# Four chained attention layers on one core: layer 2's chunks turned in 32x32 blocks, statistics in 64x64 tiles, the last chunk stored in one go

## The chip, the cores and the metric

The kernel runs on one core of one Trainium2 chip. The metric is the device time of one execution in microseconds (us). Before the change it is 2960.8 us, the median of 3 runs (2960.5 to 2961.66). One further execution was recorded by the hardware profiler; all durations and positions below come from that one.

The engines are called by their names or as the profile has them: TensorE (PE for products, PEld for weight loads), VectorE (DVE), ScalarE (ACT), GpSimd (POOL) and SyncE (SP, which issues most of the transfers). L1284 is line 1284 of the kernel before.

## The reference: what is computed

Four images x of 64x64 positions and 64 channels, all fp32, go through four attention layers, each on the result of the one before. Each has a softmax over all 4096 positions (1024 pooled ones in layer 1).

```
layer 0:  q, k, v = x Wq + bq, x Wk + bk, x Wv + bv;   x = gamma * softmax(q k^T) v + x
layer 1:  theta = x w_theta, phi, g = maxpool2(x w_phi), maxpool2(x w_g)      (spectrally normed weights)
          x = x + sigma * (softmax(theta phi^T) g w_o + b_o)
layer 2:  xn = group_norm(x, 32 groups, eps 1e-5), x read as (B, C, H, W); its last axis is projected:
          q, k, v = xn Wq^T + bq, ...;   o = softmax(q k^T / 8) v;   x = x + o Wp^T + bp
layer 3:  h = group_norm(x, 8 groups over channels, eps 1e-3)
          x = h + softmax((h wq + bq)(h wk + bk)^T / 8) (h wv + bv) wp + bp
```

## The kernel before, in words

**Tiling.** Each image is kept as a tile of 128 partitions by 2048 columns; the two halves of 64 partitions are two sets of tokens with 64 channels each. TensorE works as four tiles of 64x64. An attention layer goes over 4 chunks of queries (512 columns in each half) and, for every chunk, over 32 blocks of keys. `first(u)` in `attention` makes the scores of one block (L1249, four 64x64 products of 512 columns, into an `s` buffer of PSUM), ScalarE takes their exponentials into a `p` tile (L1254), VectorE adds the `p` tiles up for the softmax sums (`zacc`, L1260), and `then(u)` adds p times v into two accumulators (L1284). An fp32 product shows as two records in the profile, so four products are two groups of four records. There are two `s` buffers (two banks each), four accumulator banks and 14 `p` tiles.

**A chunk's end** (layers 2 and 3). VectorE transposes `zacc` in 32x32 blocks and sums it (L1268, L1272: `zsums`). ScalarE and VectorE bring the accumulators together as `o` (L1293, L1294). Two steps of pairs later `turn` runs, and four steps later `last`. In layer 2, `turn` transposes `o` by four products with the identity on the full 128x128 array (L1411), sums `zsums` over partitions by column products of 128x32 (L1414), and multiplies the turned result by the reciprocal sums on its way out of PSUM (L1419). `last` multiplies by Wp^T (L1430, 64x64 tiles) and adds bias and residual (L1435). In layer 3 there is no projection left to do (it is folded into v): `sums` makes the sums by 64x64 products (L1499), VectorE transposes `o` in 32x32 blocks (L1531), divides (L1519), adds the residual, transposed likewise (L1514, L1536), and SP stores the chunk (L1524, four stores of 64 KB).

**Statistics.** The group norms of layers 2 and 3 (`before2`, `before3`) sum over columns on VectorE, and over partitions by a product with a matrix of averages, `avg2` or `avg3`, on the full array (L1323, L1343, L1455, L1473): twice for each image and layer, 16 in all. The inverse root is taken on GpSimd (L764).

**Order.** The order of all instructions on each engine is written out by hand. `step` emits one pair of `first`, then the work that is due (`then`), and between them one piece of a background generator: the preparation of another image's layer or the whole small layer 1. `urgent` holds the turns and the last steps of chunks and goes ahead of the background. TensorE and VectorE take their instructions strictly in that order. SP takes its transfers in the order of the program: the inputs, the weights (until 47 us), then swapped copies and the next images.

**The very last chunk** (`final`, the last image's layer 3) is done in two halves of 256 columns. For each, ScalarE copies one accumulator, VectorE adds the other (L1547), transposes (L1548), divides (L1519) and adds the residual, transposed ahead of time (L1552). The first half's four stores of 32 KB go out on SP before the second half is done, the second half's on SP and ACT. In between a flag is made: all softmax sums and reciprocals are compared with bounds (`rest_in_range`, `count_bad`), a product counts partitions out of range, and every engine loads the count and branches past a general version of the kernel that is not run here.

Of the kernel before, what the change touches and what calls it, by code (L numbers as in the profile page):

```python
# [8 lines left out]
FP = mybir.dt.float32  # L9
I32 = mybir.dt.int32  # L10
AF = mybir.ActivationFunctionType
ALU = mybir.AluOpType
AX = mybir.AxisListType
# [584 lines left out]
def fast_path(tc: tile.TileContext, a: dict, out: bass.AP, bad, read_flag):  # L598
# [9 lines left out]
    nc = tc.nc  # L608
    x = a["x"]
    B, H, W, C = x.shape  # L610
    N = H * W
    P = 128
    W2 = W // 2
    S = N // 2
    NC = S // 512
    NB = N // P
# [9 lines left out]
    x_p, p_p, z_p, o_p = pool("x", 13), pool("p", 14), pool("z", 2), pool("o", 2)  # L626
    ps_s, ps_a = pool("ps_s", 2, space=PSUM), pool("ps_a", 4, space=PSUM)

    s_tile = lambda: ps_s.tile([P, 1024], FP, tag="s", name="s")
# [3 lines left out]
    o_tile = lambda name: o_p.tile([P, 512], FP, tag=name, name=name)  # L633
# [21 lines left out]
    def ctile(shape, name):  # L655
        return const.tile(shape, FP, tag=name, name=name)
# [92 lines left out]
    NCHECK = B * (NB + 2 + NC * (8 + 16))  # L749
# [3 lines left out]
    def check_columns(n):  # L753
        i = checks[0]
        checks[0] += n
        return all_z[:, i : i + n], all_r[:, i : i + n]
# [477 lines left out]
    def attention(st, turn, last, not_before, name, final=None):  # L1234
# [65 lines left out]
        start = now[0]  # L1300
# [6 lines left out]


    def before2(on, st):
# [12 lines left out]
        t = s_tile()[:, 0:G]  # L1322
        nc.tensor.matmul(t, avg2, stat, start=True, stop=True)  # L1323
        nc.vector.tensor_copy(mean, t)  # L1324
# [17 lines left out]
        t = s_tile()[:, 0:G]  # L1342
        nc.tensor.matmul(t, avg2, stat, start=True, stop=True)  # L1343
        var, rstd = small_tile("var2"), small_tile("rstd2")
        nc.vector.tensor_scalar(var, t, 1e-5, None, ALU.add)
# [57 lines left out]
    def layer2(st, not_before):  # L1403
        xv = st["x"].rearrange("p (h g e n) -> p e g n h", h=H, e=2, n=4)

        def turn(o, zsums):

            s = s_tile()
            turned, z = s[:, 0:512], s[:, 512 : 512 + 2 * 4]
            for n in range(4):  # L1410
                nc.tensor.transpose(turned[:, ds(n * P, P)], o[:, ds(n * P, P)], ident)  # L1411
            by_query = zsums.rearrange("p (i n r) -> p r n i", i=2, n=4)
            for r in range(4):
                nc.tensor.matmul(z[quarter(r), :], lanes[:, 0:32], by_query[:, r, :, :], start=True, stop=True)  # L1414
            z_columns, r_columns = check_columns(2 * 4)
            nc.vector.tensor_copy(z_columns, z)
            nc.vector.reciprocal(r_columns, z_columns)
            t = o_p.tile([P, 2 * 4, C], FP, tag="turned", name="turned")
            nc.vector.tensor_tensor(  # L1419
                t.rearrange("p (n i) f -> p n i f", n=4), turned.rearrange("p (n i f) -> p n i f", n=4, i=2),  # L1420
                r_columns.rearrange("p (n i) -> p n i", n=4).unsqueeze(3).to_broadcast([P, 4, 2, C]), ALU.mult,
            )
            return t

        def last(c, t):
            t = t.rearrange("p (i n) h -> p i n h", i=2)
            s = s_tile()
            for e in range(2):
                for i in range(2):
                    nc.tensor.matmul(  # L1430
                        s[half(i), ds(e * 512, 256)], wp2[half(e), :], t[half(e), i, :, :], start=True, stop=True
                    )
            for e in range(2):
                x_out = xv[:, e, c, :, :]
                nc.vector.scalar_tensor_tensor(  # L1435
                    x_out, s[:, ds(e * 512, 256)].rearrange("p (n h) -> p n h", h=H), bp2, x_out, ALU.add, ALU.add
                )

        return attention(st, turn, last, not_before, "done2")


    def before3(on, st):
# [11 lines left out]
        t = s_tile()[:, 0:1]  # L1454
        nc.tensor.matmul(t, avg3, sums, start=True, stop=True)  # L1455
        nc.vector.tensor_copy(mean, t)
# [15 lines left out]
        t = s_tile()[:, 0:1]  # L1472
        nc.tensor.matmul(t, avg3, sums, start=True, stop=True)  # L1473
        var, fac = col("var3"), col("fac3")
        nc.vector.tensor_scalar(var, t, 1e-3, None, ALU.add)
# [11 lines left out]
    def layer3(st, not_before):  # L1487
# [3 lines left out]
        blocked = lambda t: t.rearrange("p (b f) -> p b f", f=32)  # L1491
        dst = out[st["b"]].rearrange("(j e b) (i w) (q f) -> j e b i w q f", e=2, b=16, i=2, q=2)

        def sums(zsums):

            s = s_tile()
            for k in range(2):
                for i in range(2):
                    nc.tensor.matmul(  # L1499
                        s[half(i), ds(k * 512, 16)], lanes[half(k), :], zsums[half(k), i * 16 : i * 16 + 16],  # L1500
                        start=True, stop=True,
                    )
            z_columns, r_columns = check_columns(16)
            nc.vector.tensor_reduce(
                z_columns, s.rearrange("p (k b) -> p b k", k=2)[:, 0:16, :], AX.X, ALU.add
            )
            nc.vector.reciprocal(r_columns, z_columns)
            return z_columns, r_columns
# [8 lines left out]
        def divide(t, r):  # L1517
            n = r.shape[-1]
            nc.vector.tensor_tensor(blocked(t), blocked(t), r.unsqueeze(2).to_broadcast([P, n, 32]), ALU.mult)  # L1519

        def store(c, t, rows, queues):
            for n in range(4):
                e, q = divmod(n, 2)
                queues[n % len(queues)](  # L1524
                    dst[c // 2, e, rows, c % 2, :, q, :].rearrange("b w f -> w b f"), blocked(t[quarter(n), :])[:, rows, :]
                )

        def turn(o, zsums):
            t = o_tile("turned")
            r = sums(zsums)[1]  # L1530
            nc.vector.transpose(t, o)  # L1531
            divide(t, r)
            return t
# [5 lines left out]
        def final(acc, zsums):  # L1539

            z_columns, r_columns = sums(zsums)
            rest_in_range(z_columns, r_columns)
            t = o_tile("turned")
            for m in range(2):
                o, rows, cols = o_tile("o")[:, 0:256], slice(m * 8, m * 8 + 8), slice(m * 256, m * 256 + 256)
                nc.scalar.copy(o, acc[0][:, cols])
                nc.vector.tensor_tensor(o, o, acc[1][:, cols], ALU.add)  # L1547
                nc.vector.transpose(t[:, cols], o)  # L1548
                if m == 0:
                    set_bad = count_bad()  # L1550
                divide(t[:, cols], r_columns[:, rows])
                nc.vector.tensor_tensor(t[:, cols], t[:, cols], kept[0][:, cols], ALU.add)  # L1552
                if m == 0:
                    store(NC - 1, t, rows, [nc.sync.dma_start])
                    set_bad()
            flag.append(read_flag())
            store(NC - 1, t, slice(8, 16), [nc.sync.dma_start, nc.scalar.dma_start])
# [5 lines left out]
        return attention(st, turn, last, not_before, "done3", final if ends else None)  # L1563
# [72 lines left out]
    wv2, wp2 = w2[:, 2, :], w2[:, 3, :]  # L1636
# [26 lines left out]
    def constants():  # L1663
# [13 lines left out]
        nc.vector.tensor_copy(wvT, s[0:C, 384:512])  # L1677
        yield MID
# [199 lines left out]
```

## Time and profile before

| | |
|---|---|
| median of 3 runs | 2960.8 us |
| the profiled execution, its own time | 2960.91 us |
| its span, first instruction to last | 2959.1 us |
| TensorE busy | 2929.1 us, 99% of the span |
| VectorE, ScalarE, GpSimd busy | 1833.0, 1923.9, 34.1 us |
| TensorE's granted clock | 0.999 |
| layer 2's transposes, L1411 | 64 records, 273 ns each |
| layer 2's sums, L1414 | 128 records, 187 ns each |
| layer 2's projection, L1430 | 128 records, 376 ns each |
| layer 3's sums, L1499 | 128 records, 192 ns each |
| statistics, L1323, L1343, L1455, L1473 | 8 records each, 260 to 286 ns |

A row of the timeline is: start, length, engine, line, operation, tiles written and read, array tile and shape, and how many records were merged into it. Matmul records overlap, because four tiles work at once and the next product starts before the last one has drained; so a record's length is not what a product costs. What a step costs TensorE is read from starts: how much later the next attention product starts than it would without the step.

### The profile page before, as it was taken

What the parts mean: (1) busy time and instruction counts of PE and PEld (TensorE: products, weight loads), DVE (VectorE), ACT (ScalarE), POOL (GpSimd) and SP (SyncE); (2) the same over time, 40 slices, a digit from 0 to 9 for tenths busy, and PEclk for the clock granted to TensorE, in tenths of its full rate; (3) what the DMA queues carried; (4) which work ended last, traced back from release to release, by engine and by line L of the source; (5) the groups of instructions that cost most, each with busy time, mean ns of one, the idle gap of its engine ahead of it and who ended that gap; (6) DMA issues with size and microseconds to landing.
All of it is one profiled execution on the core that took longest, in us unless ns stands there. A gap on an engine that the chain in (4) does not pass through costs nothing.

```text
span 2959.1 us, 66032 instructions
## 1 busy us (share of the span) xinstructions
PE 2929.1 (99%) x29189; PEld 1122.1 (38%) x29189; DVE 1833.0 (62%) x2088; ACT 1923.9 (65%) x2769; POOL 34.1 (1%) x32
## 2 busy tenths in 40 slices
PE   9999999999999999999999999999999999999998
PEld 3333233333444433444443334333344344333332
DVE  1211742588721078862017887888888777878877
ACT  6877777665588866567886655655555555555554
POOL 0000000000000000000000000000000000000000
PEclk9999999999999999999999999999999999999999
DMA  2010000000002000000000000000000000000000
GB/s 38 1 30 5 1 1 16 5 1 16 2 1 30 1 5 1 16 1 16 1 1 5 2 16 2 19 5 9 5 19 6 18 1 2 8 16 5 9 5 9
DMA packets 70630, 25.87 MB, mean 9 GB/s; under 512 B 68416, under 2 KB 68416, under 8 KB 68928
## 3 DMA queue, kind: packets, MB, share of 16 engines
q1 hardware_dynamic: 68624, 21.23, 4.1%
q8 instruction: 230, 3.77, 0.5%
q10 hardware_dynamic: 1712, 0.34, 0.1%
q14 instruction: 64, 0.52, 0.1%
HBM read 4.79 MB, written 4.19 MB: 3 GB/s over the span
## 4 chain that ended last, share of the span: by engine, by line
PE 97%; ACT 1%; DVE 1%; issue 0%; DMA 0%; ACTq 0%; DVEq 0%
PE acc L1284 30%; PE s L1249 30%; PE s L994 15%; PE acc L1025 15%; PE s L1118 2%; PE acc L1144 2%; ACT p L1124 1%; PE s L1144 1%; PE s L906 0%; PE s L885 0%; PE s L1373 0%; PE s L1411 0%; PE s L1090 0%; PE s L1179 0%; DVE zacc L1260 0%
## 5 line engine op out<-in xcount | busy, mean ns | idle before, releaser
L1254 ACT ACTIVATE p<-s 128x1024 f32<-128x1024 f32 x1024 | 994.2, 1022 | 695.0 <-PE s L1249 687.0
L1260 DVE TENSOR_TENSOR zacc<-zacc,p 128x1024 f32<-128x1024 f32 x960 | 1173.6, 1223 | 304.1 <-ACT p L1254 257.1
L1284 PE MATMUL acc<-p,v 64*64 64x512 f32 (+1 forms) x8576 | 1011.8, 572 | 0.0
L1284 PEld LDWEIGHTS acc<-p,v 64*64 64x64 f32 x8576 | 339.6, 133 | 549.7 <-issue 547.4
L1025 PE MATMUL acc<-p,vs 64*64 64x512 f32 (+1 forms) x4224 | 512.4, 578 | 0.5 <-ACT vs L1014 0.5
L1004 ACT ACTIVATE p<-s 128x1024 f32<-128x1024 f32 x480 | 487.0, 1015 | 32.8 <-PE s L994 14.1
L1249 PE MATMUL s<-q,k 64*64 64x512 f32 x2048 | 491.7, 590 | 1.7 <-ACT p L1124 1.7
L994 PE MATMUL s<-xT,q 64*64 64x512 f32 x2048 | 488.1, 591 | 2.7 <-DVE mean L1324 0.6
L994 PE MATMUL s<-xT,q_swapped 64*64 64x512 f32 x2048 | 488.6, 591 | 0.7 <-DVE o L1153 0.7
L1249 PE MATMUL s<-q,xT 64*64 64x512 f32 x2048 | 487.8, 589 | 0.0
L1249 PE MATMUL s<-q,h_swapped 64*64 64x512 f32 x2048 | 479.7, 589 | 0.5 <-DVE v L1398 0.5
L1249 PE MATMUL s<-q,k_swapped 64*64 64x512 f32 x2048 | 477.4, 590 | 0.0
L1006 DVE TENSOR_REDUCE all_z<-z 128x1 f32<-128x4 f32 x128 | 20.1, 157 | 628.8 <-ACT p L1004 628.5
L1025 PEld LDWEIGHTS acc<-p,vs 64*64 64x64 f32 x4224 | 178.9, 133 | 270.3 <-issue 206.1
L1014 ACT ACTIVATE vs<-v,all_r 64x64 f32<-64x64 f32 x512 | 176.7, 345 | 142.6 <-PE acc L1025 69.9
L994 PEld LDWEIGHTS s<-xT,q_swapped 64*64 64x64 f32 x2048 | 146.2, 133 | 144.2 <-issue 113.6
L1249 PEld LDWEIGHTS s<-q,k_swapped 64*64 64x64 f32 x2048 | 146.7, 133 | 137.4 <-issue 93.3
L994 PEld LDWEIGHTS s<-xT,q 64*64 64x64 f32 x2048 | 147.3, 133 | 135.1 <-issue 104.8
L1249 PEld LDWEIGHTS s<-q,h_swapped 64*64 64x64 f32 x2048 | 144.7, 133 | 141.2 <-issue 129.9
L1249 PEld LDWEIGHTS s<-q,xT 64*64 64x64 f32 x2048 | 144.7, 133 | 138.8 <-issue 132.6
L1249 PEld LDWEIGHTS s<-q,k 64*64 64x64 f32 x2048 | 146.9, 133 | 116.7 <-issue 101.0
L1124 ACT ACTIVATE p<-s 128x1024 f32<-128x1024 f32 x128 | 124.2, 1022 | 80.8 <-PE s L1118 80.8
(227 smaller groups left out, 1315.0 us busy)
## 6 DMA issues: line engine op xcount, KB each, us to landing
k_swapped<-k SPq DMA_DIRECT2D x8, 512.0 KB, 4.8
h_swapped<-xT SPq DMA_DIRECT2D x8, 512.0 KB, 4.7
out_dram<-turned SPq DMA_DIRECT2D x60, 64.0 KB, 2.0
xin<-in_x_dram SPq DMA_DIRECT2D x12, 256.0 KB, 6.8
q_swapped<-q SPq DMA_DIRECT2D x6, 512.0 KB, 5.1
pg<-pg SPq DMA_DIRECT2D x8, 128.0 KB, 2.2
xin<-in_x_dram SPq DMA_DIRECT2D x12, 64.0 KB, 2.4
xin<-in_x_dram ACTq DMA_DIRECT2D x4, 64.0 KB, 2.7
```

Source lines behind the costliest of these rows:

```text
L994: nc.tensor.matmul(s[half(e), chunk(i)], queries(m, i, e), k[half(i), chunk(c)], start=True, stop=True)
L1004: nc.scalar.activation(p, s, AF.Exp, accum_out=z)
L1006: nc.vector.tensor_reduce(zsum[:, m : m + 1], zs.pop(m), AX.X, ALU.add)
L1014: nc.scalar.activation(vs[half(e), :], v[half(e), m, :], AF.Copy, scale=rz[half(e), m : m + 1])
L1025: nc.tensor.matmul(acc[c][half(i), cols], vs[half(e), :], ps[2 * t + n][half(e), chunk(i)][:, cols], start=(m == 0 and e == 0), stop=(m == ...
L1118: nc.tensor.matmul(ss[e][half(m), chunk(i)], pgs[0 if e == d else 1][r, ds(n * P + m * C, C)], th[r, chunk(i ^ j)], start=True, stop=True,)
L1124: nc.scalar.activation(pk[e], ss[e], AF.Exp)
L1144: nc.tensor.matmul(acc[quarter(q), :], g[:, k, :], ps[j, k][q // 2][:, chunk(q % 2)], start=(k == 0 or not bank), stop=(k == NK - 1 or not ...
L1249: nc.tensor.matmul(s[half(e), chunk(i)], k[(j + i) % 2][half(i), ds(j // 2 * P + e * C, C)], q[half(i), chunk(c)], start=True, stop=True,)
L1254: nc.scalar.activation(p, s, AF.Exp)
L1260: add = lambda: nc.vector.tensor_tensor(zaccs[c], p0, p, ALU.add)
L1284: nc.tensor.matmul(accs[c][e][half(i), cols], v[half(e), j, :], p[half(e), chunk(i)][:, cols], start=(j == 0), stop=(j == NB - 1),)
```

## The change

Layer 2's `turn` becomes layer 3's: the functions `blocked`, `sums`, `divide` and `turn` move out of `layer3` and serve both layers. `o` is no longer transposed as a whole, only within blocks of 32x32. The rest of the reordering moves into `last`: Wp^T is kept in a new constant `wp2` of 2x2 blocks, filled up with zeros for the tokens that a product must not mix, and four products of 256 columns become sixteen of 128 columns, which read the turned tile in runs of 32 and write PSUM in runs of 32. `wp2` is cleared by GpSimd and filled by eight small transfers on SP.

The products of the statistics are made by a new function `summed`: four products in 64x64 tiles into two banks, and a reduction on VectorE that adds the two banks.

In `final`, both halves are brought together and transposed first, then divided; GpSimd adds the residual of the first half, VectorE that of the second, and the whole chunk is stored at the end by four transfers of 64 KB, two on SP and two on ACT.

```diff
-    NCHECK = B * (NB + 2 + NC * (8 + 16))
+    NCHECK = B * (NB + 2 + 2 * NC * 16)
...
         st["done1"] = True
-    def attention(st, turn, last, not_before, name, final=None):
+    blocked = lambda t: t.rearrange("p (b f) -> p b f", f=32)
+
+    def sums(zsums):
+
+        s = s_tile()
+        for k in range(2):
+            for i in range(2):
+                nc.tensor.matmul(
+                    s[half(i), ds(k * 512, 16)], lanes[half(k), :], zsums[half(k), i * 16 : i * 16 + 16],
+                    start=True, stop=True,
+                )
+        z_columns, r_columns = check_columns(16)
+        nc.vector.tensor_reduce(
+            z_columns, s.rearrange("p (k b) -> p b k", k=2)[:, 0:16, :], AX.X, ALU.add
+        )
+        nc.vector.reciprocal(r_columns, z_columns)
+        return z_columns, r_columns
+
+    def divide(t, r):
+        n = r.shape[-1]
+        nc.vector.tensor_tensor(blocked(t), blocked(t), r.unsqueeze(2).to_broadcast([P, n, 32]), ALU.mult)
+
+    def turn(o, zsums):
+
+
+        t = o_tile("turned")
+        r = sums(zsums)[1]
+        nc.vector.transpose(t, o)
+        divide(t, r)
+        return t
+
+    def attention(st, last, not_before, name, final=None):
...
             step(lambda: (first(2 * t), first(2 * t + 1)))
         return 0
+    def summed(dst, w, src):
+
+        n = src.shape[-1]
+        s = s_tile()
+        for i in range(2):
+            for e in range(2):
+                nc.tensor.matmul(s[half(e), ds(i * 512, n)], w[half(i), half(e)], src[half(i), :], start=True, stop=True)
+        nc.vector.tensor_reduce(dst, s.rearrange("p (i n) -> p n i", i=2)[:, 0:n, :], AX.X, ALU.add)
+
     def before2(on, st):
...
             yield MID
             nc.vector.tensor_reduce(stat[:, gs], grouped(x2[:, sl]), AX.X, ALU.add)
         yield MID
-        t = s_tile()[:, 0:G]
-        nc.tensor.matmul(t, avg2, stat, start=True, stop=True)
-        nc.vector.tensor_copy(mean, t)
+        summed(mean, avg2, stat)
         for gs, sl in halves:
             yield MID
             nc.vector.tensor_tensor(
...
             nc.vector.tensor_reduce(stat[:, gs], grouped(xn[:, sl]), AX.X, ALU.add)
         yield MID
         yield MID
-        t = s_tile()[:, 0:G]
-        nc.tensor.matmul(t, avg2, stat, start=True, stop=True)
         var, rstd = small_tile("var2"), small_tile("rstd2")
-        nc.vector.tensor_scalar(var, t, 1e-5, None, ALU.add)
+        summed(var, avg2, stat)
+        nc.vector.tensor_scalar(var, var, 1e-5, None, ALU.add)
         yield from inverse_root(rstd, var, 3)
         fac = small.tile([P, G, 2], FP, tag="fac2", name="fac2")
         nc.vector.tensor_tensor(
...
                 )
     def layer2(st, not_before):
-        xv = st["x"].rearrange("p (h g e n) -> p e g n h", h=H, e=2, n=4)
-
-        def turn(o, zsums):
-
+        xv = st["x"].rearrange("p (h g j f) -> p g j f h", h=H, j=4, f=2)
+
+        def last(c, t):
+
+            t = t.rearrange("p (i a e n h) -> p i n e a h", i=2, a=2, e=2, n=2)
             s = s_tile()
-            turned, z = s[:, 0:512], s[:, 512 : 512 + 2 * 4]
-            for n in range(4):
-                nc.tensor.transpose(turned[:, ds(n * P, P)], o[:, ds(n * P, P)], ident)
-            by_query = zsums.rearrange("p (i n r) -> p r n i", i=2, n=4)
-            for r in range(4):
-                nc.tensor.matmul(z[quarter(r), :], lanes[:, 0:32], by_query[:, r, :, :], start=True, stop=True)
-            z_columns, r_columns = check_columns(2 * 4)
-            nc.vector.tensor_copy(z_columns, z)
-            nc.vector.reciprocal(r_columns, z_columns)
-            t = o_p.tile([P, 2 * 4, C], FP, tag="turned", name="turned")
-            nc.vector.tensor_tensor(
-                t.rearrange("p (n i) f -> p n i f", n=4), turned.rearrange("p (n i f) -> p n i f", n=4, i=2),
-                r_columns.rearrange("p (n i) -> p n i", n=4).unsqueeze(3).to_broadcast([P, 4, 2, C]), ALU.mult,
-            )
-            return t
-
-        def last(c, t):
-            t = t.rearrange("p (i n) h -> p i n h", i=2)
-            s = s_tile()
-            for e in range(2):
-                for i in range(2):
-                    nc.tensor.matmul(
-                        s[half(i), ds(e * 512, 256)], wp2[half(e), :], t[half(e), i, :, :], start=True, stop=True
-                    )
-            for e in range(2):
-                x_out = xv[:, e, c, :, :]
+            for m in range(2):
+                for n in range(2):
+                    for f in range(2):
+                        for i in range(2):
+                            nc.tensor.matmul(
+                                s[half(i), ds(f * 512, 256)].rearrange("p (j h) -> p j h", h=H)[:, :, m * 32 : m * 32 + 32],
+                                wp2[half(f), m, n, :], t[half(f), i, n, :, :, :], start=(n == 0), stop=(n == 1),
+                            )
+            for f in range(2):
+                x_out = xv[:, c, :, f, :]
                 nc.vector.scalar_tensor_tensor(
-                    x_out, s[:, ds(e * 512, 256)].rearrange("p (n h) -> p n h", h=H), bp2, x_out, ALU.add, ALU.add
+                    x_out, s[:, ds(f * 512, 256)].rearrange("p (j h) -> p j h", h=H), bp2, x_out, ALU.add, ALU.add
                 )
-        return attention(st, turn, last, not_before, "done2")
+        return attention(st, last, not_before, "done2")
     def before3(on, st):
...
             z_columns, r_columns = sums(zsums)
             rest_in_range(z_columns, r_columns)
             t = o_tile("turned")
-            for m in range(2):
-                o, rows, cols = o_tile("o")[:, 0:256], slice(m * 8, m * 8 + 8), slice(m * 256, m * 256 + 256)
+            parts = [slice(m * 256, m * 256 + 256) for m in range(2)]
+            for m, cols in enumerate(parts):
+                o = o_tile("o")[:, 0:256]
                 nc.scalar.copy(o, acc[0][:, cols])
                 nc.vector.tensor_tensor(o, o, acc[1][:, cols], ALU.add)
                 nc.vector.transpose(t[:, cols], o)
                 if m == 0:
                     set_bad = count_bad()
-                divide(t[:, cols], r_columns[:, rows])
-                nc.vector.tensor_tensor(t[:, cols], t[:, cols], kept[0][:, cols], ALU.add)
+            for m, cols in enumerate(parts):
+                divide(t[:, cols], r_columns[:, m * 8 : m * 8 + 8])
                 if m == 0:
-                    store(NC - 1, t, rows, [nc.sync.dma_start])
                     set_bad()
+                engine = nc.gpsimd if m == 0 else nc.vector
+                engine.tensor_tensor(t[:, cols], t[:, cols], kept[0][:, cols], ALU.add)
             flag.append(read_flag())
-            store(NC - 1, t, slice(8, 16), [nc.sync.dma_start, nc.scalar.dma_start])
+            store(NC - 1, t, slice(0, 16), [nc.sync.dma_start, nc.scalar.dma_start])
         kept = []
         ends = st["b"] == B - 1
         if ends:
             before.setdefault(now[0] + NC * NB // 2 - 8, []).append(lambda: later.append(lambda: kept.append(residual(NC - 1))))
-        return attention(st, turn, last, not_before, "done3", final if ends else None)
+        return attention(st, last, not_before, "done3", final if ends else None)
     def alone(*phases):
...
             load[0](wl2[:, i, j, :], a["L2_conv_" + n])
     w2 = ctile([P, 4, C], "w2")
     wqk2 = w2[:, 0:2, :].rearrange("p i f -> p (i f)")
-    wv2, wp2 = w2[:, 2, :], w2[:, 3, :]
+    wv2 = w2[:, 2, :]
+
+    wp2 = ctile([P, 2, 2, C], "wp2")
+    nc.gpsimd.memset(wp2, 0.0)
...
         nc.vector.tensor_scalar(w2[:, 0, :], w2[:, 0, :], 0.125, None, ALU.mult)
         nc.vector.tensor_copy(wvT, s[0:C, 384:512])
+        for q in range(4):
+            for n in range(2):
+                nc.sync.dma_start(wp2[quarter(q), q % 2, n, :], w2[quarter(n), 3, :])
         yield MID
         form_transposes(3, s_tile())
         yield MID
```

`before3` changes as `before2` does (L1455, L1473), and in `layer3` the moved functions go.

More of the change, by code (lines that the diff above doesn't have):

```diff
@@ L1453, in before3 @@
         yield MID
-        t = s_tile()[:, 0:1]
-        nc.tensor.matmul(t, avg3, sums, start=True, stop=True)
-        nc.vector.tensor_copy(mean, t)
+        summed(mean, avg3, sums)
         sq = x_tile("sq")
@@ L1471, in before3 @@
         yield MID
-        t = s_tile()[:, 0:1]
-        nc.tensor.matmul(t, avg3, sums, start=True, stop=True)
         var, fac = col("var3"), col("fac3")
-        nc.vector.tensor_scalar(var, t, 1e-3, None, ALU.add)
+        summed(var, avg3, sums)
+        nc.vector.tensor_scalar(var, var, 1e-3, None, ALU.add)
         yield from inverse_root(fac, var, 2)
@@ L1490, in layer3 @@
         h = st.pop("x"), st["k"][1]
-        blocked = lambda t: t.rearrange("p (b f) -> p b f", f=32)
         dst = out[st["b"]].rearrange("(j e b) (i w) (q f) -> j e b i w q f", e=2, b=16, i=2, q=2)
[L1494 to L1508, printed above, removed]
         def residual(c):
@@ L1515, in residual @@
             return t
-        def divide(t, r):
-            n = r.shape[-1]
-            nc.vector.tensor_tensor(blocked(t), blocked(t), r.unsqueeze(2).to_broadcast([P, n, 32]), ALU.mult)
         def store(c, t, rows, queues):
@@ L1526, in store @@
                 )
[L1528 to L1533, printed above, removed]
         def last(c, t):
```

## The prediction

> **What bounds the kernel now.** I read the page first: its busy shares and its chain of waits.
>
> ```profile
> PE 2929.1 (99%) x29189; PEld 1122.1 (38%) x29189; DVE 1833.0 (62%) x2088; ACT 1923.9 (65%) x2769; POOL 34.1 (1%) x32
> PE 97%; ACT 1%; DVE 1%; issue 0%; DMA 0%; ACTq 0%; DVEq 0%
> ```
>
> TensorE is busy 99% of the span and carries 97% of the chain that ended last. Its granted clock is 0.999. A step off TensorE counts only where TensorE waits for it, or after its last product. So I read, in the timeline of TensorE, what each inserted step adds between two attention products. Plain attention runs in pairs of groups, x8, that start 0.86 us apart (640.94 to 641.80 below).
>
> Layer 2's turn (L1411, L1414), full-array transposes and column products:
>
> ```profile
> 630.94 1.04 PE L1284 MATMUL acc<-p,v 64*64 64x512 f32 x8
> 631.91 0.66 PE L1411 MATMUL s<-ident,o 128*128 128x128 f32 x4
> 632.50 0.25 PE L1414 MATMUL s<-zsums,lanes 128*32 128x8 f32 x8
> 632.68 1.09 PE L1284 MATMUL acc<-p,v 64*64 64x512 f32 x8
> ```
>
> From pair to pair 1.74 instead of 0.86. The pair behind it is slower too: the next products start at 633.59, 0.91 after 632.68, so 0.05 more. The turn costs 0.93 us.
>
> Layer 2's last products (L1430), and the products of layer 3's sums (L1499), which stay in 64x64 tiles:
>
> ```profile
> 640.94 1.04 PE L1284 MATMUL acc<-p,v 64*64 64x512 f32 x8
> 641.80 0.61 PE L1430 MATMUL s<-turned,w 64*64 64x256 f32 x8
> 642.23 1.04 PE L1284 MATMUL acc<-p,v 64*64 64x512 f32 x8
> ```
>
> ```profile
> 1884.06 1.04 PE L1284 MATMUL acc<-p,v 64*64 64x512 f32 x8
> 1884.92 0.25 PE L1499 MATMUL s<-zsums,lanes 64*64 64x16 f32 x8
> 1885.01 1.07 PE L1284 MATMUL acc<-p,v 64*64 64x512 f32 x8
> ```
>
> L1430 costs 642.23 - 641.80 = 0.43. L1499 costs 0.09, and 0.03 in the pair behind it (next start 1885.90): 0.12 us.
>
> A statistics product on the whole array (L1455), and the group most like the new last products (L1373: 32 records of 128 columns):
>
> ```profile
> 1734.69 1.07 PE L1284 MATMUL acc<-p,v 64*64 64x512 f32 x8
> 1735.69 0.38 PE L1455 MATMUL s<-sums,avg 128*128 128x1 f32 x2
> 1736.00 1.09 PE L1284 MATMUL acc<-p,v 64*64 64x512 f32 x8
> ```
>
> ```profile
> 496.52 1.05 PE L1373 MATMUL s<-w,xn 64*64 64x128 f32 x32
> 497.40 0.61 PE L1025 MATMUL acc<-p,vs 64*64 64x512 f32 x4
> ```
>
> L1455: 1.31 - 0.86 = 0.45, and 0.05 behind it (next start 1736.91): 0.50. L1373: 0.88, or 0.11 for each of its eight groups of four.
>
> Last I read the end: the stores, and one GpSimd row.
>
> ```profile
> 2951.15 3.62 SPq L1524 DMA_DIRECT2D out_dram<-turned  x4
> 2951.31 0.42 DVE L1552 TENSOR_TENSOR turned<-turned,residual 128x256 f32<-128x256 f32 x1
> 2951.77 1.38 ACTq L1524 DMA_DIRECT2D out_dram<-turned  x2
> ```
>
> ```profile
> 1751.09 1.23 DVE L1260 TENSOR_TENSOR zacc<-zacc,p 128x1024 f32<-128x1024 f32 x1
> 1751.14 1.59 POOL L764 TENSOR_TENSOR fac<-var,minus_half 128x1 f32<-128x1 f32 x1 [388.49 <-DVE var L1475]
> ```
>
> The last arithmetic ends at 2951.73, but SP's fourth store of the first half takes 1.63 us to issue, so SP's last two go out at 2953.8 and 2954.2 and land by 2957.5. The span ends 1.6 later, at 2959.1.
>
> **The change, part by part.**
>
> *Layer 2's turn, 16 times.* Four transposes and four column products go; four 64x16 products, those of L1499, come. 0.93 - 0.12 = 0.81, times 16: **13.0 us less**. It is all on TensorE's path: attention stands on both sides. VectorE loses a copy (0.17), a reciprocal (0.20) and a multiply out of PSUM (0.69), and gains a reduction (0.18), a longer reciprocal (0.25), a transpose (0.70) and a multiply (0.69): 0.77 more per chunk. I cost that at nothing. The cover is VectorE's idle time: busy 117.14 of 140.00 us (576 to 716) and 95.09 of 106.00 (2066 to 2172). Layer 3 does these steps and a 2.1 us residual besides (two transposes of 0.70, an add of 0.69) without stopping TensorE. If the cover were gone: 16 x 0.77 = 12.3. VectorE still waits once for the product of sums; behind it are the zacc adds, and behind those only the 14 p buffers. The s buffer comes free after the small reduction instead of after the multiply, so the next scores wait no longer than now.
>
> *Layer 2's last products, 16 times.* Four products of 256 columns become sixteen of 128: eight groups of four, as in L1373. 0.88 - 0.43 = 0.45, times 16: **7.2 us more**. Two things are not in any row: moving data in 32-element runs, and PSUM outputs in runs of 32 with gaps of 32. Lower bound 0.11 a group (L1373); upper bound 0.43, the start distance of two 512-column attention groups, as if every run cost a whole product. I take 0.11, the row with the same columns and tiles. The two adds (L1435, 0.69 each) follow as now; the scores behind them are later by the same amount.
>
> [...]
>
> *Statistics, 16 products.* Each becomes four 64x64 products like L1499. Fourteen save 0.50 - 0.12 = 0.38: 5.3. In the other two TensorE waits for VectorE's mean to free s (0.3 us each in the list of waits) and before that for ScalarE; those waits stay, and I give them 0.25 each. **5.8 us less.** On VectorE copies become reductions of equal length (0.18), plus eight small adds, beside other work.
>
> *At no cost.* GpSimd's memset of wp2 (0.2 to 0.4 us; it idles 84 us before 88.7). Eight small DMAs on SP wait for w2 (58.3 us) and take about 0.6 each to issue, as their neighbours do; SP has nothing between 47 and 158 us, where q_swapped and the next input queue behind them. If they held those up it would be at most 5 us, once. The 632 instead of 504 check columns add 0.5 us to VectorE long before the end.
>
> *The last chunk.* On VectorE 2.57 us lie between 2949.16 and 2951.73 in the chain; one add (0.45 with its issue) leaves, so it would be done at 2951.3. GpSimd's add of 128x256: rows L1603 (128x64, 318 ns) and L1813 (128x16, 221 ns) give 2.0 ns per column, so I estimate 0.70. Beside VectorE's multiply and add it would end by 2951.3 too; waiting for them, at 2952.0. I take 2952.0, since L764 above ran on 0.4 us past the end of the VectorE operation that began just before it, all four times, while four columns alone took 1.03.
>
> [...]
>
> Then four stores of 64 KB, two on SP and two on ACT, where eight of 32 KB went. The second goes out about 0.4 later and lands 2.0 (64 KB, median) to 3.5 (the slowest of the last eight) after that: 2954.4 to 2955.9. I take 2955.4, nearer the late end, since the last three stores of before all needed 3.2 to 3.5. Against 2957.5 that is **2.0 us less**. Bounds: 3.5 less (2951.3 and 2.0), or 0.5 more if the stores stall as SP's fourth did (2952.0 + 0.4 + 1.6 + 3.5 = 2957.5, and something for double the size).
>
> *Sum.* 13.0 - 7.2 + 5.8 + 2.0 = 13.6. The profiled execution took 2960.91 (span 2959.1 and 1.8 around it); 2960.91 - 13.6 = 2947.3; it stood 0.1 above the median of the runs, so **2947.2**.
>
> **Rivals.**
> *A: the end gives nothing or costs.* GpSimd blocks, stores of double size come at once and land late: +0.5 instead of -2.0, 2949.7. For it: SP's 1.63 us issue. Against: the queue then held four stores more.
> *B: VectorE becomes the bound.* The full 12.3 come back on TensorE: 2959.5; half of it: 2953.4. For it: 90% busy in one stage. Against: layer 3's chunks, which are heavier.
> *C: the strided last products are slow, and the kernel gets slower.* Place: the 128 groups of the last products. The gain of 13.6 is used up when a group costs 0.11 more (0.22), and it is slower by over 0.2% from 0.26. At the upper bound of 0.43: 128 x 0.32 = 41 more, 2988. Against: nothing in L1373 hints at it.
> That the full-array products stay is excluded: in the changed program they are replaced one for one and TensorE's order is otherwise the same.
>
> **How the numbers follow.** 0.2% is 5.9 us, about what a measurement of this kernel can tell from no change. Forecast: 0.66 (2945.3 to 2949). A: 0.18. B, in part or whole: 0.08 (2950 to 2960). C: 0.08. The range holds the forecast, A and a little of B: 2945.0 (the end at its best) to 2952.0. Faster: 0.66 + 0.18 + half of B and a little of C = 0.89. Same: 0.05. Slower: 0.06.
>
> **What would show it.** Right: L1411 and L1414 gone, the new sums within 0.15 us between attention pairs, the sixteen last products in 0.85 to 0.95, statistics without a full-array form, TensorE's last attention product 11 to 12 us earlier. Wrong: last products over 1.7 us; new waits of TensorE for VectorE in layer 2; GpSimd's add past 2 us, or stores that land over 4 us after issue. A stall of 1.4 us that TensorE shows as "issue" at 165 us may move with the program's length.

## The result and the profile after

The changed kernel takes **2947.74 us** (median of 6 runs, 2947.57 to 2948.7) against 2960.62 us for the kernel before (6 runs on the same chip, 2959.73 to 2961.66): ratio 0.9957, 95% interval 0.9944 to 0.9970, or 12.9 us less. Forecast were 2947.2. The profiled execution took 2947.80 us, its span 2946.0, at a granted clock of 0.999 as before.

The page of the changed kernel, busy time of the engines and the chain that ended last by engine:

```profile
PE 2916.9 (99%) x29605; PEld 1131.8 (38%) x29605; DVE 1844.3 (63%) x2111; ACT 1924.0 (65%) x2769; POOL 34.7 (1%) x34
PE 97%; DVE 2%; ACT 1%; issue 0%; DVEq 0%; ACTq 0%
```

TensorE still bounds the kernel and is busy 12.2 us less; VectorE has 11.3 us more. What the new steps add between two attention products is read from the timeline of TensorE, as in the prediction (start, length, engine, line, tiles; L1315 is now p times v, L1280 the scores; dots stand for rows left out):

```profile
630.40 0.25 PE L1241 MATMUL s<-zsums,lanes 64*64 64x16 f32 x8
630.49 1.07 PE L1315 MATMUL acc<-p,v 64*64 64x512 f32 x8
631.38 0.59 PE L1280 MATMUL s<-q,k 64*64 64x512 f32 x2
...
639.59 1.05 PE L1451 MATMUL s<-turned,wp 64*64 64x128 f32 x32
640.46 1.04 PE L1315 MATMUL acc<-p,v 64*64 64x512 f32 x8
641.32 0.59 PE L1280 MATMUL s<-q,k 64*64 64x512 f32 x2
```

```profile
1728.25 0.24 PE L1345 MATMUL s<-sums,avg 64*64 64x1 f32 x8
1728.33 1.07 PE L1315 MATMUL acc<-p,v 64*64 64x512 f32 x8
1729.22 0.60 PE L1280 MATMUL s<-q,k 64*64 64x512 f32 x2
```

The sums of layer 2 (L1241) cost 0.09 and 0.03 in the pair behind them. The sixteen last products (L1451) cost 640.46 - 639.59 = 0.87, and no more behind them (0.86 to the next start). A statistics product (L1345) costs 0.08 + 0.03.

The attention products come in the same order in both programs, 25,088 records. So I matched them one to one and took the difference of their starts; each place where that difference changes is a place where time was won or lost. The last attention product starts at 2946.42 before and at 2933.63 after, **12.79 us** earlier:

| where the difference changes | us won | forecast |
|---|---|---|
| layer 2's turn, 16 places, and the pairs behind them | 12.77 - 0.23 = 12.54 | 13.0 |
| layer 2's last products, 16 places | -6.79 | -7.2 |
| statistics, 16 products | 5.43 | 5.8 |
| an "issue" stall at 165 us | 0.71 | "may move" |
| waits at other places, net, and rounding | 0.90 | 0 |
| **TensorE's last attention product** | **12.79** | **11.6** |
| from its start to the end of the span: 12.70 before, 12.36 after | 0.34 | 2.0 |

The end gave almost nothing. The last adds and the stores in the timeline of the changed kernel, and the transfers of its last 8 us (queue, kind: packets, MB, share of 16 engines; then issues with their median time to landing):

```profile
2937.62 0.84 POOL L1548 TENSOR_TENSOR turned<-turned,residual 128x256 f32<-128x256 f32 x1 [1.45 <-DVE bad L1818]
2937.91 0.83 DVE L1548 TENSOR_TENSOR turned<-turned,residual 128x256 f32<-128x256 f32 x1
2938.81 1.95 SPq L1522 DMA_DIRECT2D out_dram<-turned  x2
2938.82 1.93 ACTq L1522 DMA_DIRECT2D out_dram<-turned  x2
```

```profile
q14 instruction: 6, 0.05, 1.7%
q8 instruction: 2, 0.03, 1.4%
...
out_dram<-turned SPq DMA_DIRECT2D x2, 64.0 KB, 3.9
out_dram<-turned ACTq DMA_DIRECT2D x2, 64.0 KB, 4.2
```

The arithmetic ends 2.37 us after `least` (L1815), where before it was 2.57 (L1816). But on both queues the second store needs over 1.5 us to issue, and the last landing comes 5.79 us after the last arithmetic, as before (5.73). The second stores, 64 KB each, land 5.2 and 5.3 us after their issue. Two queues that carry instructions move packets while the stores run.

### The profile page after: what moved, and what is told of

Same layout as the page of the kernel before. It is cut to its first block, busy times and chain, and to the rows that moved or that the text cites. A ratio compares the mean times of both kernels' runs of the same rounds, so it can differ in the third digit from the quotient of the medians.

```text
span 2946.0 us, 66890 instructions
## 1 busy us (share of the span) xinstructions
PE 2916.9 (99%) x29605; PEld 1131.8 (38%) x29605; DVE 1844.3 (63%) x2111; ACT 1924.0 (65%) x2769; POOL 34.7 (1%) x34
## 4 chain that ended last, share of the span: by engine, by line
PE 97%; DVE 2%; ACT 1%; issue 0%; DVEq 0%; ACTq 0%
PE acc L1315 29%; PE s L1280 29%; PE s L994 15%; PE acc L1025 15%; PE s L1118 2%; PE acc L1144 2%; DVE zacc L1291 1%; ACT p L1124 1%; PE s L1144 1%; PE s L906 0%; PE s L885 0%; PE s L1410 0%; PE s L1451 0%; PE s L1179 0%; PE s L1090 0%
## 5 line engine op out<-in xcount | busy, mean ns | idle before, releaser
L1315 PE MATMUL acc<-p,v 64*64 64x512 f32 (+1 forms) x8576 | 1008.6, 572 | 0.0
L1315 PEld LDWEIGHTS acc<-p,v 64*64 64x64 f32 x8576 | 338.1, 133 | 548.6 <-issue 548.6
L1280 PE MATMUL s<-q,k 64*64 64x512 f32 x2048 | 490.4, 590 | 1.7 <-ACT p L1124 1.7
L1280 PE MATMUL s<-q,xT 64*64 64x512 f32 x2048 | 488.3, 589 | 0.0
L1280 PE MATMUL s<-q,h_swapped 64*64 64x512 f32 x2048 | 479.6, 589 | 0.8 <-DVE v L1435 0.5
L1280 PE MATMUL s<-q,k_swapped 64*64 64x512 f32 x2048 | 476.7, 590 | 0.1
L1280 PEld LDWEIGHTS s<-q,h_swapped 64*64 64x64 f32 x2048 | 145.1, 133 | 141.0 <-issue 128.0
L1280 PEld LDWEIGHTS s<-q,k_swapped 64*64 64x64 f32 x2048 | 145.6, 133 | 137.9 <-issue 91.4
L1280 PEld LDWEIGHTS s<-q,xT 64*64 64x64 f32 x2048 | 145.2, 133 | 138.1 <-issue 130.4
L1280 PEld LDWEIGHTS s<-q,k 64*64 64x64 f32 x2048 | 146.0, 133 | 117.7 <-issue 100.1
```

Source lines behind the costliest of these rows:

```text
L1280: nc.tensor.matmul(s[half(e), chunk(i)], k[(j + i) % 2][half(i), ds(j // 2 * P + e * C, C)], q[half(i), chunk(c)], start=True, stop=True,)
L1315: nc.tensor.matmul(accs[c][e][half(i), cols], v[half(e), j, :], p[half(e), chunk(i)][:, cols], start=(j == 0), stop=(j == NB - 1),)
```

## The experiments

Two questions were open: which part brought what, and why the end gave nothing. A third came up on the way: whether VectorE's cover in layer 2 is as wide as the prediction said.

**One part each.** Layer 2's turn and last products alone, the statistics alone, the new end alone, each put into the kernel before; and the changed kernel with VectorE adding both halves of the last residual:

```diff
-                engine = nc.gpsimd if m == 0 else nc.vector
-                engine.tensor_tensor(t[:, cols], t[:, cols], kept[0][:, cols], ALU.add)
+                nc.vector.tensor_tensor(t[:, cols], t[:, cols], kept[0][:, cols], ALU.add)
```

> Layer 2's chunks alone are changed (turn, last, wp2, the longer list of checks); statistics and the last chunk as before. Theory from TensorE's starts: sixteen turns save 0.80 us each and sixteen last products cost 0.44 more, so 5.7 us less than before, to which 0.9 us of shorter waits behind the last products may come: 2954 to 2955 us. Rival (VectorE's 0.77 us per chunk comes back on TensorE): 12 us more than that, about 2966. Rival (runs of 32 in PSUM slow the products): over 1.7 us for each last step.

> Only the sixteen products of the statistics go to 64x64 tiles. Theory: 0.38 us saved for each of fourteen, little for two, 5.4 us less: about 2955.3. Rival (the full array's switch is hidden behind the reductions, nothing is saved): 2960.7. If the stall of 1.4 us at 165 us of the span is due to where the instructions lie, it may be shorter or longer here, by up to 0.8.

> Only the last chunk is changed. The prediction's step: 2.0 us less, 2958.7. Theory from the two traces: arithmetic 0.2 us shorter, landings just as late after it, so 0.3 us less, 2960.4, inside what can be told from before. Its profile should again show VectorE's last add at about 0.84 instead of 0.42 us, and the stores' landing over 5 us after their issue.

> The changed kernel, but VectorE adds the residual of both halves of the last chunk. If GpSimd and VectorE take turns at the data, GpSimd's half is worth nothing: arithmetic ends within 0.1 us of the changed kernel's and the time is the same, 2947.7. If they ran beside each other, the arithmetic would end 0.4 us later: 2948.1.

The kernel before took 2961.25 us beside these four. The changed kernel was not run again beside the experiments; the kernel before was, with medians of 2960.61 to 2961.25, which ties the series together to 0.6 us.

| kernel | median us | ratio, 95% interval | last attention product, us earlier |
|---|---|---|---|
| layer 2's part | 2951.81 | 0.9969, 0.9957 to 0.9981 | 7.58 |
| statistics | 2957.07 | 0.9985, 0.9976 to 0.9994 | 2.95 |
| the new end | 2960.27 | 0.9999, 0.9990 to 1.0008 | -0.75 |
| changed, VectorE adds both | 2947.70 | 0.9958, 0.9944 to 0.9971 | 12.42 |

Layer 2's part won 12.81 - 0.23 at the turns and lost 6.79 at the last products, as the whole change does (12.77 - 0.23 and 6.79). Its time is over 2 us below the 2954 to 2955 expected: 0.8 of its 7.58 us come from the stall at 165 us, and its span ends 11.63 us after that last product's start, 1.07 sooner than in the kernel before, though its end is the old one. The statistics won 5.47 at their sixteen places, but the products that this edit doesn't touch lost 2.5 of it: 1.2 in the first 170 us, 0.7 in a new stall at 741 us, and small steps; so 2957.07 instead of the 2955.3 expected. Other programs here show such shifts too (see the last section); they are why the parts don't add up to better than a microsecond or two. The new end alone is within the noise of no change, as the theory had it; the prediction's own step would have given 2958.7.

With VectorE adding both halves, the timeline shows the two adds one by one:

```profile
2937.89 0.43 DVE L1547 TENSOR_TENSOR turned<-turned,residual 128x256 f32<-128x256 f32 x1
2938.23 0.42 DVE L1254 TENSOR_TENSOR turned<-turned,all_r 128x256 f32<-128x256 f32 x1
2938.68 0.42 DVE L1547 TENSOR_TENSOR turned<-turned,residual 128x256 f32<-128x256 f32 x1
```

VectorE's adds (L1547) take 0.43 and 0.42, where its own add beside GpSimd's took 0.83. The arithmetic ends 2.37 us after `least` in both kernels, and the times agree. GpSimd's half is worth nothing: what VectorE is spared, it loses again on its own half (0.83 instead of 0.42). What makes that add longer is not shown. If VectorE had only begun when GpSimd was through, its add would end 0.42 after GpSimd's, and it ends 0.28 after it (2938.74 against 2938.46).

**What holds the end.** The engines load the flag and branch past the general version; the theory is that the code behind the branch must then be fetched, and that this is what the two instruction queues above carry. One kernel leaves the branch out of the changed kernel, the other out of the kernel before; in both the flag is computed, no engine reads it, and the general version is gone from the program.

```diff
-        n_bad = fast_path(tc, a, out, bad, lambda: nc.values_load(
-            bad[0:1, 0:1], min_val=0, max_val=128, skip_runtime_bounds_check_because="it is a count of 128 partitions"
-        ))
-        with tc.If(n_bad > 0):
-            general_path(tc, a, out)
+        fast_path(tc, a, out, bad, lambda: None)
```

> The changed kernel without the branch at its end: the flag is still computed, but no engine reads it, and the general path behind it is left out of the program. Theory (the engines' jump past the general path and the code it makes them fetch are what holds back the second stores and the last landings): the second stores issue in about 0.5 us instead of 1.5, the last store lands at most 3.5 us after the last arithmetic instead of 5.8, so 2 to 3 us less than the changed kernel, 2944.7 to 2945.7. Rival (four stores of 64 KB in 128-byte pieces need that long by themselves): the last landing stays over 5 us after the last arithmetic, and the time within 1 us of the changed kernel's 2947.7, less what the shorter end of the program saves.

> The kernel before without the branch at its end and the general path behind it; the flag is computed and not read. It asks whether the old end, too, is held back by the branch, and what the new end would be worth without it. Theory (the branch and the fetches behind it set the last landing, whatever the stores are): the span ends about 3 us earlier, 2957.5 to 2958.5, with the last landing 3.3 to 4 us after the last arithmetic instead of 5.7, and against the changed kernel without the branch (2945.9) the end's own worth is below 1 us. Rival (my prediction's 2.0 us was real and the branch hid it): the old end lands 5 us or more after the arithmetic even without the branch, 2959.5 to 2960.6.

The changed kernel without the branch took 2945.92 us (2945.4 to 2945.94, 5 runs), the kernel before without it 2957.5 us (2955.19 to 2958.17, 10 runs; 2960.61 with it). The first is 0.2 us above the range expected, with TensorE's last attention product 0.89 us later than in the changed kernel (2934.52 against 2933.63). The stores of the changed kernel without the branch, in the timeline and in the transfers of its last 5 us, in which no instruction queue appears any more:

```profile
2939.69 0.85 SPq L1522 DMA_DIRECT2D out_dram<-turned  x2
2939.70 0.92 ACTq L1522 DMA_DIRECT2D out_dram<-turned  x2
```

```profile
q10 hardware_dynamic: 1056, 0.13, 15.6%
q1 hardware_dynamic: 1056, 0.13, 14.8%
...
out_dram<-turned SPq DMA_DIRECT2D x2, 64.0 KB, 2.6
out_dram<-turned ACTq DMA_DIRECT2D x2, 64.0 KB, 2.8
```

The same of the kernel before without the branch:

```profile
2948.07 3.04 SPq L1524 DMA_DIRECT2D out_dram<-turned  x6
2949.86 0.84 ACTq L1524 DMA_DIRECT2D out_dram<-turned  x2
```

```profile
q14 instruction: 1, 0.01, 0.7%
...
out_dram<-turned SPq DMA_DIRECT2D x4, 32.0 KB, 1.9
out_dram<-turned ACTq DMA_DIRECT2D x2, 32.0 KB, 1.8
```

| from the end of `zsums` on | before | after | before, no branch | after, no branch |
|---|---|---|---|---|
| last arithmetic to last landing, us | 5.73 | 5.79 | 2.17 | 3.27 |
| `zsums` to the end of the span, us | 11.84 | 11.49 | 8.10 | 8.41 |

These are single profiles, and with the branch the end varies from program to program: from `zsums` to the end of the span, the four profiles with the old end have 10.03 to 11.84, and the six with the new end and the flag set as late 10.28 to 11.49. So the branch and what goes with it cost 1.9 to 3.7 us at the old end and 1.9 to 3.1 at the new one (3.1 and 1.8 in the medians). Without it the old end is no slower than the new one, in these two profiles 0.3 us faster: its small stores land in 1.8 to 1.9 us, the large ones in 2.6 to 2.8, and half of its data leaves early. The late landings of the old end, from which the prediction drew its 2.0 us, were not the eight stores' own. The two packets of queue 8 (0.03 MB) in the last 8 us are gone without the branch, which fits the theory; that they are the code behind the branch is not shown. The flag's load, the branch and the general version went out together, so these runs don't tell which of them counts, nor whether the landings wait for these packets or for transfer engines that the packets keep busy.

A kernel that sets the flag about 0.7 us earlier, and so branches earlier (VectorE adds both halves, as in the kernel above that took 2947.70):

```diff
+                if m == 1:
+                    set_bad()
...
-                if m == 0:
-                    set_bad()
```

> The changed kernel with VectorE adding both halves of the last residual, and the flag's last step moved ahead of the second half's transpose, so that the engines branch about 0.7 us earlier. Theory (the landings hang on when the engines have passed the branch): 0.4 to 0.8 us less than the changed kernel, 2947.0. Rival (they hang on when the data is ready and on the stores alone): the same 2947.7.

It took 2946.86 us (2945.78 to 2947.46, 5 runs) against 2961.01: ratio 0.9952, 0.9939 to 0.9966. The theory's size and sign, but the interval overlaps that of the changed kernel, so it is not shown.

**VectorE's cover in layer 2.** The new turn with the old last products, and the changed kernel with VectorE's transpose done twice or not at all:

```diff
         nc.vector.transpose(t, o)
+        if name == "done2":
+            nc.vector.transpose(t, o)
```

> Layer 2's new turn with the old last products: four products of 256 columns that read the tokens in the new order as if it were the old one, so layer 2 puts out other numbers than the reference; layer 3 works on as before. Against the run with layer 2's part whole (2951.8) this prices the sixteen products alone. Theory (eight groups of 0.11 instead of four products of 0.43 in all, runs of 32 cost nothing, and what they cost lies wholly on TensorE): 7 us less than that run, 2944.8, or up to 1 us more than that where waits behind the products come back. Rival (the sixteen products cost more than their records show, through the strided output or later waits): 10 us less or more.

> The changed kernel with VectorE's transpose in layer 2's turn done twice, 16 times 0.70 us more of VectorE's time, the same result. Theory (VectorE's idle time covers the new turn with room to spare): within 1.5 us of the changed kernel, 2947.7 to 2949.2. Rival (VectorE is near its limit in layer 2, so what is added there comes back on TensorE): half to all of the 11.2 us, 2953.3 to 2958.9.

> The changed kernel without VectorE's transpose in layer 2's turn (the multiply reads the sum of the accumulators itself, so layer 2 puts out other numbers than the reference): 16 times 0.70 us less of VectorE's time. With the second transpose the time was 5.8 us more. Theory (VectorE's cover in layer 2 is just about used up by the changed kernel): taking 0.70 away brings only the waits that the changed kernel shows for VectorE in layer 2, about 0.8 us, so 2946.5 to 2947.7. Rival (VectorE's time counts by half all along, and the changed kernel already pays for its own part): 4 to 6 us less, 2942 to 2944.

| kernel | median us | last attention product against | us |
|---|---|---|---|
| new turn, old last products | 2950.24 | layer 2's part | 2.34 earlier |
| transpose twice | 2953.5 | the changed kernel | 6.22 later |
| no transpose | 2947.32 | the changed kernel | 0.45 earlier |

I expected 7 us for the sixteen products and got 1.6 of the medians, 2.3 of the starts. They do cost 7.03 at their own places. But with the short products 4.05 come back as waits (another 0.9 go to the stall at 165 us). More VectorE time in the turn costs just over half of what it is, as the rival had it (5.8 of 11.2 us); less of it gains 0.4, within the spread of the runs, so the changed kernel pays next to nothing for its turn on VectorE. Where the waits arise is told by the adds that follow the last products: what VectorE waited for before them, and who waited for them. The changed kernel first, then the new turn with the old products, then the doubled transpose:

```profile
L1457 DVE SCALAR_TENSOR_TENSOR xT<-s,bp,xT x32: 655/696/723, 640.7 to 2507.1; 128x256 f32<-128x256 f32 x32
its engine sat idle before it (us, times) until:
  PE s L1451: 2.2, 9
who waited for it (us, times):
  PE s L1280: 0.2, 1
```

```profile
L1446 DVE SCALAR_TENSOR_TENSOR xT<-s,bp,xT x32: 643/698/761, 642.6 to 2509.2; 128x256 f32<-128x256 f32 x32
...
who waited for it (us, times):
  PE s L1280: 1.9, 5
```

```profile
L1459 DVE SCALAR_TENSOR_TENSOR xT<-s,bp,xT x32: 648/694/710, 642.1 to 2513.3; 128x256 f32<-128x256 f32 x32
its engine sat idle before it (us, times) until:
  PE s L1453: 0.2, 1
who waited for it (us, times):
  PE s L1282: 3.4, 5
```

In the changed kernel VectorE arrives at these adds a little ahead of the products (idle 2.2 us in 9 places), in the other two behind them, since it adds `zacc` first; the `s` buffer stays taken and the scores wait. (The view lists only the longer waits.) One such place with the doubled transpose, on VectorE and then TensorE:

```profile
640.93 1.22 DVE L1293 TENSOR_TENSOR zacc<-zacc,p 128x1024 f32<-128x1024 f32 x1
...
642.06 1.27 DVE L1459 SCALAR_TENSOR_TENSOR xT<-s,bp,xT 128x256 f32<-128x256 f32 x2
...
643.48 0.65 PE L1282 MATMUL s<-q,k_swapped 64*64 64x512 f32 x2 [0.55 <-DVE xT L1459]
```

The last products are through by 641.2, the adds run from 642.06 to 643.33, and the scores start at 643.48 after 0.55 us of idling. Is that VectorE's load, or the place of the adds in its queue? The last kernels call layer 2's last products two steps later, once with the early flag and once with the doubled transpose:

```diff
-                urgent.append((now[0] + 4, lambda: last(c, os.pop(c))))
+                urgent.append((now[0] + (6 if name == "done2" else 4), lambda: last(c, os.pop(c))))
```

> The variant with the early flag and VectorE's two adds, and layer 2's last products called two steps later, six steps after the chunk's accumulators end instead of four. Theory (the waits for VectorE at the last products come from its queue at that moment, not from its load as a whole): the small waits go or move, 0 to 0.8 us less than 2946.9. Rival (the later call meets another pass of VectorE): up to 2 us more.

> The changed kernel with VectorE's transpose in layer 2's turn done twice, and the last products called two steps later. Theory (TensorE waits because the adds that free the scores' buffers stand in VectorE's queue behind what the turn has delayed, and two steps later it has caught up): most of the 5.8 us of the doubled transpose go, 2948 to 2949.5. Rival (VectorE is at its limit over the whole chunk, wherever the products stand): 2952 to 2954, as with the doubled transpose alone.

The doubled transpose with the later call took 2949.19 us (2947.75 to 2950.14, 5 runs) instead of 2953.5, so 4.3 of the 5.8 us went; VectorE waits for the products again, and nobody waits for the adds:

```profile
L1459 DVE SCALAR_TENSOR_TENSOR xT<-s,bp,xT x32: 656/699/727, 651.8 to 2514.1; 128x256 f32<-128x256 f32 x32
its engine sat idle before it (us, times) until:
  PE s L1453: 3.2, 11
who waited for it (us, times):
```

TensorE's last attention product starts only 0.66 us later than in the kernel with the later call and the early flag (2935.07 against 2934.41; the medians differ by 2.65), for the same 11.2 us of VectorE's time that cost 6.22 with the early call. So it is mostly the place in the queue: VectorE has the time, but not at that moment. The later call with the early flag took 2946.54 us (2945.84 to 2947.25, 4 runs) against 2960.61: ratio 0.9951, 0.9934 to 0.9967. It has the lowest median of the kernels that keep the branch, though it can't be told from the changed kernel by these runs.

## Why the prediction was right, point by point

The time was forecast to 0.5 us, but that closeness is luck: two errors of over a microsecond cancelled.

- **The turn, 16 x 0.81.** Right: 12.54 measured, 0.78 each. The sums cost 0.12 as in layer 3.
- **The last products, 16 x 0.45.** Right at their own places: 6.79, 0.42 each. The row chosen (L1373, 0.11 a group) was the right one: eight groups in 0.87. Rival C falls: with runs of 32 fp32 values read from SBUF and written to PSUM with gaps, the products show no slowdown (0.87 against 0.88 for eight groups of L1373).
- **The statistics, 5.8.** 5.43 in the whole change, 5.47 alone. Right.
- **"I cost that at nothing"**, VectorE's 0.77 more in each turn. Right for this kernel, for the wrong reason. The busy share (117 of 140 us) and the comparison with layer 3 don't show the cover: layer 3 has no product behind its turn whose buffer VectorE must free. What covered the longer turn was the longer step behind it, priced in the same prediction: with the old, shorter products, 4.05 us return as waits, a part of rival B. The net price of the sixteen products is thus 2 to 3 us, and 0.70 us more in each turn would have cost 5.8. The new waits that the prediction named as a sign against itself are there, but small: 0.2 us in the list of waits, three steps of 0.1 to 0.4 in the matched starts.
- **Not in the sum:** 0.71 us from the shorter stall at 165 us, which the prediction named without a price, and 0.90 from other waits. They make TensorE's gain 12.8 instead of 11.6, beyond the "11 to 12" given as a sign.
- **The last chunk, 2.0 less.** Wrong: 0.34 in the profiled executions. In four profiles with the old end, the last attention product starts 10.9 to 12.7 us before the span's end, in six with the new one (and the flag set as late) 11.1 to 12.4, so the end's gain is nothing that can be measured. The 2.0 were drawn from one profile, whose end is the longest of the four. The failed step is "I take 2955.4", the landing 3.4 us after the last arithmetic. It was 5.8. The arithmetic itself ended 0.5 earlier against `least` than assumed. The prediction read the old end's slow stores as queueing, so that fewer stores would bring it forward; they were slow because of the branch and what goes with it, which stay. Only without the branch does the last store land as forecast (3.27), and then the old end's lands after 2.17. Rival A, given 0.18, is what happened at the end: VectorE's add is held up beside GpSimd's (0.83 instead of 0.42), and the sign "land over 4 us after issue" came true (5.2 and 5.3). Only its price was 0.3 less instead of 0.5 more, and the double size that it blamed accounts for 0.8 us of a landing (2.6 to 2.8 against 1.8 to 1.9 without the branch); the rest is gone without the branch.
- **At no cost** (the memset, eight transfers, more check columns): no wait of TensorE for them shows.

## What to carry to other kernels

An engine's busy share doesn't show whether a longer step on it is free (here VectorE was busy 117 of 140 us, and 0.70 us more in each of sixteen turns cost 5.8): look at the moment in its queue where it frees a buffer for the bounding engine, and shift that moment before making the step shorter. When stores at the end of a program land late, take out what else happens there before changing the stores (here the flag's load, the branch and the general version: without them the last landing came 2.17 and 3.27 us after the last arithmetic instead of 5.73 and 5.79). Price a step together with the one behind it: here the longer products hid 4.05 us of waits that the new turn had brought with its longer time on VectorE.

## What the runs showed of the hardware

- The flag's load and the taken branch past the general version at the program's end, taken out together with that version, cost 1.9 to 3.7 us from the last `zsums` to the span's end (10.0 to 11.8 with them, 8.10 and 8.41 without). In the medians it is 3.1 for the kernel before and 1.8 for the changed one.
- A VectorE add of 128x256 beside a GpSimd add of the same shape (0.84) took 0.83 in the changed kernel; alone, with both adds on VectorE, it took 0.42.
- Between attention products, one statistics product of one column cost 0.11 as four products in 64x64 tiles (L1345) and 0.50 on the whole array (L1455 of the kernel before).
- The first microseconds differed between two programs that are the same there: in the profiled execution of the kernel before without the branch, TensorE's first sixteen records of L885 start at 8.1 to 9.4 us instead of 9.5 to 12.1, the next of that line at 24.3 instead of 26.5, and its last at 2597.8 instead of 2599.7, so 1.9 us earlier still. That execution took 2955.19 us where its kernel's median is 2957.5, so here differences of a microsecond are read from matched products, not from spans.
